# A hand-ordered selective scan: two copies moved behind the scans of their group, and the states of two tiles dealt anew among the engines

## The chip, the cores and the metric

The kernel runs on one core of a Trainium2 chip. The metric is the device time of one execution in microseconds (us); lower is better. The time stated for a kernel is the median of several executions.

## The reference

The network has four layers on a tensor of 4 images x 64 x 64 positions x 96 channels. Layers 0 and 1 are the costly ones: a group norm, an input projection to 192 + 192 channels, a depthwise 3x3 convolution with SiLU, a selective scan over the 4096 positions in four directions k, and a gated output projection. Layers 2 and 3 are linear attention and a small quantised feed-forward net on tokens.

The change lies in the selective scan. Cut to one image and one direction it computes, for 192 channels d and 16 states n:

```
x_dbl = xs @ x_proj_weight.T          # dts (6 ranks), B (16), C (16) of each position
delta = softplus(dts @ dt_w.T + bias)
for l in positions:                   # the recurrence, along the free dimension
    h[d, n] = exp(delta[l, d] * A[d, n]) * h[d, n] + delta[l, d] * u[l, d] * B[l, n]
    y[l, d] = sum_n h[d, n] * C[l, n]
y += D * u
```

## The kernel before

**Units, chunks, tiles, groups.** A unit is one layer and a pair of images; there are four units, one after another. The 2 x 192 channels of a pair are held as three tiles of 128 partitions: tile 0 and tile 1 are the first 128 channels of each image, tile 2 holds the last 64 of both. The 4096 positions of a direction are cut into four chunks of T = 1024, so a unit has 4 directions x 4 chunks = 16 chunks, and a chunk has three tiles. `steps` lists (k, ci, j): direction, chunk, tile. The 16 states of a tile are worked in groups of NG = 2, so a tile has eight groups, with n0 = 0, 2, ..., 14, and a chunk 24.

**What one state costs.** The scan itself is one VectorE (DVE) instruction over 1024 positions, which needs the decay `da` = exp(delta x A) from ScalarE (ACT), and the input `bp` = delta x u x B, in PSUM. Who makes `bp` is set for each tile and state by a letter of `MAKERS`:

- A: ACT scales the eight 128x128 blocks of the transposed delta x u (`dut`) by B (function `outer`, the tile `x`; in tile 2 sixteen blocks of 64 columns), and TensorE (PE) transposes them into `bp`.
- V: PE spreads B over the partitions with two selection matmuls (`bp<-bparts,sel`), and DVE multiplies `bp` by `du` in place just ahead of the scan.
- G: B is spread by a DMA (`bb`), GpSimd (POOL) multiplies it by `du` into `dbu`, and ACT writes the decay into `bp` instead (`exp_of`, held back in `late` to the next group's start).

After the scan POOL copies the last state where a later chunk follows (`last`), and multiplies h by C, which a DMA has spread (`cb`, three buffers, 1 MB a group). PE then transposes the products and adds them up in PSUM (`add_up`, `yp`), LAG = 3 groups later.

**The order.** Four engines run in program order, which is written out by hand in the loop over groups of `scan`. At group g it is: `bp` of the group's second state, the sum of group g - 3, ACT's work for group g + 1 (`start_ahead`: `x` and `da`; buffers: `x` 2, `da` 4, `bp` 2, `h` 4), the scan of the first state, the first `bp` of group g + 1, the scan of the second state, then the pieces that are due, then POOL's copies and products.

**The pieces.** The next chunk's projection (`project`, into the rows `cdt` and `crow`, and B in `bt` and `bparts`), the softplus of its deltas (`soften`) and the next tile's `du` and `dut` (`discretise`) are generators. Each yields the place at which its next piece is due, and `drive` runs the pieces of the place that has come. A projection's places are (tile, n0). In tiles 0 and 1 it makes one half of 512 positions each: a matmul `xps` at n0 = 8, 10 and 12, and at n0 = 14 ACT's copy of `xps` to `cdt` (76x512); behind the second copy the `crow` rows are written to memory. In tile 2 it turns B, and ends with ACT's copy `bparts` at n0 = 14. The places of `discretise` are 6, 8, 10 and 12.

`drive` is called behind the scans of each group. In the group with n0 = 14 it is also called once ahead of `start_ahead`, for `discretising` and `projecting`, so the last piece of a tile's projection stands ahead of ACT's work for the next tile's first group.

All engine instructions are recorded by one helper, so the profile shows them all under L61; they are told apart by their tiles.

Of the kernel before, what the change touches and what calls it, by code (L numbers as in the profile page):

```python
# [25 lines left out]
NS = 16  # L26
# [8 lines left out]
NG = 2  # L35
LAG = 3

MAKERS = ("VAAAVAAGVAVVAAVA", "AAVAVAVAAGAVAVAA", "VAVAVGVVVAVGVVAA")
NT = L // 128
STARTS = (0, 26, 52, 77)  # L40
HID = 4 * C
# [86 lines left out]
class Rounds:  # L128
# [7 lines left out]
    def run(self):  # L136
        for r in range(max(self.tasks) + 1):
            for task, args in self.tasks.get(r, ()):
                task(*args)
            yield  # L140

def between_scans(tc, cst, ident, half, pn, u, before, scan, after):

    with ExitStack() as stage:
# [374 lines left out]
def load_weights(nc, pk, w, k):  # L519

    wx = pk.tile([128, 3, NC], F32, name="wx")
    nc.sync.dma_start(out=wx, in_=w["wx"][k])
    wdt = pk.tile([NC, 3, 128], F32, name="wdt")
    nc.sync.dma_start(out=wdt, in_=w["wdt"][k])
    return wx, wdt

class PairScan:
# [129 lines left out]
    def scan(self, stage, nc):  # L657
# [9 lines left out]
        def begin_project(k, ci):  # L667
            return self.project(nc, nc.gpsimd, odd if ci % 2 else self.pq, pm, "m1", k, ci)

        def begin_discretise(at):  # L670
            return self.discretise(nc, nc.gpsimd, odd if at % 2 else self.pq, pm, "m0", at)

        def begin_soften(ats):
            return self.soften(nc, [self.pq, odd, odd, odd], pm, [("m0", "m1"), ("yp",), ("m0", "m1")], ats)
# [8 lines left out]
        def drive(pieces, place):  # L683

            while pieces and pieces[0] == place:
                pieces[0] = next(pieces[1])
# [4 lines left out]
        def maker(g, i):  # L691
            at, n0 = groups[g]
            return MAKERS[steps[at][2]][n0 + i]

# [7 lines left out]
        def start_ahead(g):  # L702

            at, n0 = groups[g]
            das, xs = {}, {}
            for i in range(NG):
                if maker(g, i) == "A":
                    xs[i] = outer(g, i)
                if maker(g, i) != "G":
                    das[i] = p2.tile([128, T], F32, name="da", bufs=4)  # L710
                    exp_of(das[i], g, i)
                if i == 0 and late:
                    exp_of(*late.pop())
            return das, xs
# [13 lines left out]
        def start_cb(g):  # L728

            at, n0 = groups[g]  # L730
            cb = p2.tile([128, NG, T], F32, name="cb", bufs=3)
            spread(cb, projected[at // 3][2], steps[at][2], n0)
            return cb
# [3 lines left out]
        def start_bb(g):  # L737

            at, n0 = groups[g]
            for i in range(NG):  # L740
                if maker(g, i) == "G":
                    bbs[g, i] = p2.tile([128, 1, T], F32, name="bb", bufs=1)
                    spread(bbs[g, i], projected[at // 3][2], steps[at][2], 2 * NS + n0 + i)

        def start_dbu(g):
            out = {}
            for i in range(NG):
                if (g, i) in bbs:
                    out[i] = p2.tile([128, T], F32, name="dbu", bufs=1)
                    nc.gpsimd.tensor_tensor(out[i], made[groups[g][0]][1], bbs.pop((g, i))[:, 0], ALU.mult)  # L750
            return out

        def start_bp(g, i, xs):

            at, n0 = groups[g]
            _, _, j = steps[at]
            bp = pm.tile([128, T], F32, name="bp", bufs=2)
            if maker(g, i) == "G":
                if g + 1 < len(groups):
                    late.append((bp, g, i))  # L760
                else:
                    exp_of(bp, g, i)
            elif maker(g, i) == "A":
                for t in range(T // 128):
                    nc.tensor.transpose(bp[:, 128 * t : 128 * t + 128], xs[i][:, t], ident)
            else:
                chosen = sel[:, n0 + i]
                if j < 2:
                    chosen = chosen[:, D1 * j : D1 * j + 1].to_broadcast([NP, 128])
                for hf in range(2):  # L770
                    cols = slice(512 * hf, 512 * hf + 512)
                    nc.tensor.matmul(
                        bp[:, cols],
                        chosen,
                        projected[at // 3][1][:, cols],
                        start=True,
                        stop=True,
                    )
            return bp
# [47 lines left out]
        def load_kept(at):  # L827

            if steps[at][0]:
                kept[at] = p2.tile([128, T // 128, 128], F32, name="kept", bufs=1)  # L830
                for tile_, there in places(at, kept[at]):
                    nc.sync.dma_start(out=tile_, in_=there)

        def finish_sum(at):
            tile_ = self.pq.tile([128, T // 128, 128], F32, name="ysum", bufs=1)
            nc.scalar.copy(tile_, sums.pop(at))
            for tile_, there in places(at, tile_):
                nc.sync.dma_start(out=there, in_=tile_)
# [6 lines left out]
        def sum_of(g):  # L845
            for i in range(NG):
                add_up(g, i, hs[g])
            del hs[g]

        def begun(pieces):  # L850
            return [next(pieces), pieces]

        for g, (at, n0) in enumerate(groups):
            k, ci, j = steps[at]
            rev, first, final = k >= 2, ci == 0, ci == L // T - 1
            if n0 == 0:
                if first and j == 0:
                    last = [pk.tile([128, NS], F32, name=f"last{i}", tag=f"last{i}") for i in range(3)]
                    for then in ORDER[ORDER.index(k) + 1 :][:1]:
                        weights[then] = load_weights(nc, pk, w, then)  # L860
                if j == 0:
                    projecting = begun(begin_project(*steps[at + 3][:2])) if at + 3 < len(steps) else []
                ahead_of = range(at + 1, min(at + (4 if at else 3), len(steps)))
                softening = begun(begin_soften(ahead_of)) if ahead_of and (j == 2 or at == 0) else []
                discretising = begun(begin_discretise(at + 1)) if at + 1 < len(steps) else []
            if n0 == 8 and at + 1 < len(steps):
                load_kept(at + 1)
            (da, xs), cb, dbu = ahead, cb_next, dbu_next
            if g + 2 < len(groups):
                start_bb(g + 2)  # L870


            def scan_one(i):
                if maker(g, i) == "V":
                    nc.vector.tensor_tensor(bps[i], made[at][1], bps[i], ALU.mult)
                way = slice(None, None, -1) if rev else slice(None)
                nc.vector.tensor_tensor_scan(
                    h[:, i, way],
                    (da[i] if i in da else bps[i])[:, way],
                    (bps[i] if i in da else dbu[i])[:, way],  # L880
                    0.0 if first else last[j][:, n0 + i : n0 + i + 1],
                    ALU.mult,
                    ALU.add,
                )

            bps = [bp_next, start_bp(g, 1, xs)]
            if g >= LAG:
                sum_of(g - LAG)
            if n0 == NS - NG:
                drive(discretising, n0)  # L890
                drive(projecting, (j, n0))
            if g + 1 < len(groups):
                ahead, cb_next, dbu_next = start_ahead(g + 1), start_cb(g + 1), start_dbu(g + 1)
            hs[g] = h = p2.tile([128, NG, T], F32, name="h", bufs=LAG + 1)
            scan_one(0)
            if g + 1 < len(groups):
                bp_next = start_bp(g + 1, 0, ahead[1])
            scan_one(1)
            drive(discretising, n0)
            if n0 == NG * (LAG - 1) and at > 0:  # L900
                finish_sum(at - 1)
            drive(softening, n0)
            drive(projecting, (j, n0))
            if not final:
                nc.gpsimd.tensor_copy(last[j][:, n0 : n0 + NG], h[:, :, 0] if rev else h[:, :, T - 1])
            for i in range(NG):
                nc.gpsimd.tensor_tensor(h[:, i], h[:, i], cb[:, i], ALU.mult)
# [445 lines left out]
```

## Time and profile before

| | |
|---|---|
| median of 3 executions | 10014.68 us (9996.38 to 10015.51) |
| the profiled execution | 10004.74 us, span 10003.0 us |
| granted TensorE clock | 0.93 of full speed |
| scan stretches of the four units | 2188.9, 2192.5, 2188.9, 2197.5 us |
| stretches before, between and after them | 172.3, 187.1, 186.2, 178.1, 511.5 us |
| chain that ended last, by engine | ACT 44%, PE 20%, DVE 18%, issue 13%, POOL 4% |

An engine's busy time is the union of its instructions. The groups of instructions give, behind the bar, busy us and the mean ns of one, and then the idle time of the engine just before them with what ended it. A mean of instructions that overlap (ACT's, PE's) is longer than the distance from one start to the next. PE is the matmuls, PEld the weight loads.

### The profile page before, as it was taken

Reading aid. Unit: us, or ns where it says so; the run is one execution under the profiler, and the core shown is the slowest. Engines: PE = TensorE matmul, PEld = TensorE weight load, DVE = VectorE, ACT = ScalarE, POOL = GpSimd, SP = SyncE. Lnnn points to the kernel's source line nnn. Section 1 sums busy time; section 2 is a strip of 40 time slices with the busy share of each in tenths; the row PEclk is TensorE's granted clock in tenths of the full one; section 3 lists DMA queues with packets and bytes.
Section 4 is the critical chain, followed back from the end, with each engine's and each line's share of the span. In section 5 each row is a group of like instructions: output and inputs, shape, how many; then the busy total and the mean of one; then the engine's idle time right before and its main releaser. Section 6 shows DMA issues by size and latency. Waiting matters only on the chain.

```text
span 10003.0 us, 148154 instructions
## 1 busy us (share of the span) xinstructions
PE 7800.2 (78%) x49548; PEld 5838.4 (58%) x49548; DVE 9336.2 (93%) x6794; ACT 9103.3 (91%) x21129; POOL 9004.9 (90%) x5362
## 2 busy tenths in 40 slices
PE   7778877777778888777877887777777888777766
PEld 4665655555566555555466555655566655555565
DVE  8999999998999999999899999999899999999957
ACT  6999999998899999998899999999899999999877
POOL 2999999996899999999599999999689999999946
PEclk8999999999899999999899999999989999999988
DMA  3777777776577877777577777777757777777730
GB/s 123 216 219 225 226 224 225 226 230 201 183 214 221 226 226 226 227 222 221 171 215 216 224 228 225 226 227 225 205 190 218 214 225 224 225 228 224 221 95 26
DMA packets 893171, 2083.68 MB, mean 208 GB/s; under 512 B 328278, under 2 KB 637848, under 8 KB 694776
## 3 DMA queue, kind: packets, MB, share of 16 engines
q1 hardware_dynamic: 892408, 2074.20, 70.7%
q8 instruction: 395, 6.47, 0.3%
q14 instruction: 368, 3.01, 0.1%
HBM read 1912.47 MB, written 161.48 MB: 207 GB/s over the span
## 4 chain that ended last, share of the span: by engine, by line
ACT 44%; PE 20%; DVE 18%; issue 13%; POOL 4%; DMA 1%; SPq 0%; DVEq 0%; ACTq 0%; POOLq 0%
ACT x L61 21%; ACT da L61 13%; DVE h L61 11%; PE yp L61 8%; PE bp L61 5%; DVE bp L61 4%; PE xps L61 3%; POOL h L61 2%; PE dps L61 2%; DVE vps L61 1%; ACT bp L61 1%; ACT ysum L61 1%; POOL du L61 1%; PE dpss L61 1%; ACT delta L61 1%
## 5 line engine op out<-in xcount | busy, mean ns | idle before, releaser
L61 POOL TENSOR_TENSOR h<-h,cb 128x1024 f32<-128x1024 f32 x3072 | 7197.0, 2369 | 165.8 <-DVE h L61 25.6
L61 DVE TENSOR_TENSOR_SCAN h<-da,last,bp 128x1024 f32<-128x1024 f32 x2112 | 4839.0, 2334 | 115.2 <-PE bp L61 7.5
L61 ACT ACTIVATE x<-dut,bt 128x128 f32<-128x128 f32 x14848 | 4225.5, 375 | 0.5 <-PE bp L61 0.3
L61 ACT ACTIVATE da<-delta,amat 128x1024 f32<-128x1024 f32 x2816 | 3150.9, 1144 | 17.4 <-DVE h L61 14.0
L61 PE MATMUL yp<-ident,h 128*128 128x128 f32 x24576 | 3156.2, 285 | 0.0
L61 PEld LDWEIGHTS yp<-ident,h 128*128 128x128 f32 x24576 | 2968.3, 148 | 210.0 <-issue 139.4
L61 PE MATMUL bp<-ident,x 128*128 128x128 f32 x12288 | 1779.2, 289 | 1210.2 <-DVE h L61 864.6
L61 PEld LDWEIGHTS bp<-ident,x 128*128 128x128 f32 x12288 | 1427.8, 147 | 1833.2 <-ACT x L61 1171.4
L61 DVE TENSOR_TENSOR bp<-du,bp 128x1024 f32<-128x1024 f32 x1280 | 1547.8, 1209 | 119.5 <-PE bp L61 119.3
L61 DVE TENSOR_TENSOR_SCAN h<-da,bp 128x1024 f32<-128x1024 f32 x704 | 1573.6, 2274 | 67.6 <-ACT da L61 19.7
L61 PE MATMUL bp<-bparts,sel 96*128 96x512 bf16 x2560 | 820.9, 404 | 559.5 <-DVE h L61 557.0
L61 PEld LDWEIGHTS <-sel 96*128 96x128 bf16 x2560 | 214.9, 101 | 937.4 <-DVE h L61 624.9
L61 POOL TENSOR_TENSOR dbu<-du,bb 128x1024 f32<-128x1024 f32 x256 | 606.6, 2370 | 0.0
L61 PE MATMUL xps<-u,wx 128*76 128x512 f32 x768 | 559.5, 814 | 0.0
L61 ACT ACTIVATE bp<-delta,amat 128x1024 f32<-128x1024 f32 x256 | 284.9, 1113 | 261.1 <-DVE h L61 261.1
L61 POOL TENSOR_TENSOR du<-delta,u 128x1024 f32<-128x1024 f32 x188 | 496.4, 2641 | 0.0
L61 DVE TENSOR_TENSOR_SCAN h<-bp,last,dbu 128x1024 f32<-128x1024 f32 x192 | 447.5, 2331 | 7.6 <-ACT bp L61 5.8
L61 POOL COPY last<-h 128x2 f32<-128x2 f32 x1152 | 217.3, 189 | 261.4 <-DVE h L61 156.0
L61 DVE SCALAR_TENSOR_TENSOR vps<-img,par,vps 128x512 f32<-128x512 f32 x520 | 387.0, 752 | 44.7 <-ACT vps L61 29.9
L61 PE MATMUL yp<-kept,ident 128*128 128x512 f32 x576 | 353.4, 747 | 65.2 <-ACT ysum L61 65.2
L61 PE MATMUL dups<-ident,du 128*128 128x128 f32 x1536 | 240.9, 280 | 63.9 <-POOL du L61 49.5
L61 ACT COPY ysum<-yp 128x1024 f32<-128x1024 f32 x192 | 192.4, 1002 | 101.3 <-PE yp L61 101.2
(146 smaller groups left out, 6092.8 us busy)
## 6 DMA issues: line engine op xcount, KB each, us to landing
cb<-crow SPq DMA_DIRECT2D x1024, 1024.0 KB
cb<-crow SPq DMA_DIRECT2D x1024, 512.0 KB
bb<-crow SPq DMA_DIRECT2D x128, 512.0 KB
bb<-crow SPq DMA_DIRECT2D x256, 256.0 KB
y<-ysum SPq DMA_DIRECT2D x192, 256.0 KB
kept<-y SPq DMA_DIRECT2D x160, 256.0 KB
y<-ysum SPq DMA_DIRECT2D x64, 512.0 KB
zt<-zg SPq DMA_DIRECT2D x64, 384.0 KB
```

What stands on the lines that cost most here:

```text
L61: return self.tc.keep_in_program_order(getattr(self.engine, op)(*args, **kwargs))
```

## The change

The copies of `cdt` in tiles 0 and 1 at n0 = 14 are no longer made ahead of `start_ahead`, but by the `drive` behind the scans of the same group. In tile 2 the early call for the projection stays. The early call for `discretising` goes. Two strings of `MAKERS` change: in tile 0 the two V of states 10 and 11 trade places with the two A of states 12 and 13, the counts staying at 9 A, 6 V, 1 G; in tile 1 the letters are dealt anew, from 10 A, 5 V, 1 G to 11 A, 4 V, 1 G. In groups of two states:

```
tile 0 before  VA AA VA AG VA VV AA VA
tile 0 after   VA AA VA AG VA AA VV VA
tile 1 before  AA VA VA VA AG AV AV AA
tile 1 after   VA AA VA AV AG AV AA AA
```

```diff
-MAKERS = ("VAAAVAAGVAVVAAVA", "AAVAVAVAAGAVAVAA", "VAVAVGVVVAVGVVAA")
+MAKERS = ("VAAAVAAGVAAAVVVA", "VAAAVAAVAGAVAAAA", "VAVAVGVVVAVGVVAA")
...
             bps = [bp_next, start_bp(g, 1, xs)]
             if g >= LAG:
                 sum_of(g - LAG)
-            if n0 == NS - NG:
-                drive(discretising, n0)
+            if j == 2 and n0 == NS - NG:
                 drive(projecting, (j, n0))
             if g + 1 < len(groups):
                 ahead, cb_next, dbu_next = start_ahead(g + 1), start_cb(g + 1), start_dbu(g + 1)
```

## The prediction

> **What bounds the kernel now.** I read four views: the page's busy line, the busy time in four consecutive chunks (stretches), the groups of instructions by shape, and the timelines of ACT, DVE and POOL around one wait.
>
> ```profile
> PE 7800.2 (78%) x49548; PEld 5838.4 (58%) x49548; DVE 9336.2 (93%) x6794; ACT 9103.3 (91%) x21129; POOL 9004.9 (90%) x5362
> ```
>
> Three engines are over 90% busy, so the page alone names no bound. The four scan stretches take 2188.9 to 2197.5 us each, 8768 of the 10003.0 us of the span, and hold all that the change touches. Four chunks (one direction) of the third one, from the first POOL product of one chunk to that of the next:
>
> ```profile
> core 0: us, PE busy (x) PEld busy (x) DVE busy (x) ACT busy (x) POOL busy (x), PEclk, DMA share, GB/s
> 5481.70:5617.90 136.20, 109.53 (x694) 79.62 (x694) 130.09 (x70) 128.34 (x303) 134.09 (x80) 0.95 0.75 219
> 5617.90:5755.20 137.30, 109.66 (x694) 80.33 (x694) 132.90 (x70) 128.97 (x306) 134.18 (x81) 0.95 0.79 224
> 5755.20:5891.40 136.20, 108.47 (x692) 79.85 (x690) 132.04 (x69) 128.02 (x302) 133.97 (x80) 0.95 0.77 226
> 5891.40:6028.30 136.90, 110.16 (x694) 82.22 (x695) 133.36 (x71) 129.24 (x306) 130.42 (x59) 0.94 0.81 233
> ```
>
> In the first three chunks POOL is busy all but 2 to 3 us, which is some 80 instructions with 0.03 us between them: **POOL is full there**. In the fourth, the last of a direction, POOL has no copies of last states (24 x 0.19 us less) and is idle 6.5 us; DVE with 133.4 busy sets the pace. How POOL waits there:
>
> ```profile
> 5471.28 7.02 POOL L61 TENSOR_TENSOR h<-h,cb 128x1024 f32<-128x1024 f32 x3 [0.87 <-DVE h L61]
> 5481.47 0.18 POOL L61 COPY last<-h 128x2 f32<-128x2 f32 x1 [3.17 <-DVE h L61]
> ```
>
> So POOL and DVE take turns: DVE's scans run 0.3 to 5 us ahead of POOL's products, and the lead is used up at two places of a chunk, tile 1 state 4 and the end of tile 2. ACT is ahead of both, and loses time like this at the end of tiles 0 and 1 (in brackets: idle before, and what ended it):
>
> ```profile
> 3132.34 0.58 ACT L61 COPY dut<-dups 128x512 f32<-128x512 f32 x1
> 3135.47 0.58 ACT L61 COPY cdt<-xps 76x512 f32<-76x512 f32 x1 [2.55 <-PE xps L61]
> 3135.95 2.45 ACT L61 ACTIVATE x<-dut,bt 128x128 f32<-128x128 f32 x8
> ```
>
> The eight x activations behind the copy needed nothing from PE. The groups give the prices and the sum of that wait:
>
> ```profile
> L61 POOL TENSOR_TENSOR h<-h,cb 128x1024 f32<-128x1024 f32 x3072 | 7197.0, 2369 | 165.8 <-DVE h L61 25.6 <-issue 21.8 <-DMA cb<-crow 9.6
> ...
> L61 ACT ACTIVATE da<-delta,amat 128x1024 f32<-128x1024 f32 x2816 | 3150.9, 1144 | 17.4 <-DVE h L61 14.0 <-POOL gn_norm L61 2.6
> L61 ACT ACTIVATE x<-dut,bt 128x128 f32<-128x128 f32 x9728 | 2970.8, 395 | 0.5 <-PE bp L61 0.3
> ...
> L61 DVE TENSOR_TENSOR bp<-du,bp 128x1024 f32<-128x1024 f32 x1280 | 1547.8, 1209 | 119.5 <-PE bp L61 119.3
> ...
> L61 ACT COPY cdt<-xps 76x512 f32<-76x512 f32 x128 | 74.5, 582 | 222.0 <-PE xps L61 222.0
> ```
>
> **What the Trainium skill says.** "PSUM — Partial Sum Buffer", section "Engine vs sequencer instructions": ScalarE's, VectorE's and GpSimd's queues are strict FIFO. The trace agrees: the x activations above stood 2.55 us behind a copy that they don't depend on. "ScalarE: Activation LUTs", section "What ACT_TABLE_LOAD costs": an activation with one pointer operand takes about 280 + 0.833 N ns, and neighbours overlap by 93; for N = 128 I estimate 294 ns from start to start, 2.35 us for eight. The trace agrees: 3135.95 to 3138.30, 2.35 us. "SBUF — State Buffer", section "Who interferes with whom": a VectorE instruction with at most one input in SBUF does not contend with GpSimd. DVE's product and scan each read one of their two tensors from PSUM here. The trace agrees: all 3072 POOL products lie between 2336 and 2495 ns. So fewer DVE products make POOL's no shorter.
>
> **The change, part by part.** There are 64 chunks (4 units of 16).
> 1. *The copy of cdt in tiles 0 and 1* goes behind the next group's ACT work. Removed: waits of 222.0 us, 3.5 a chunk (117 of 128 copies waited). A wait is put in its place only if PE's xps is later than the next group's ACT work, and that includes a da whose buffer (ring of four) is freed by the scan of state 13; xps stands ahead of that. I take 0. Bounds: 3.5 saved, none saved. Behind the later copy in tile 1 stand the write of crow (SP) and the dps matmuls (PE, two groups on, about 10 us). The write went out at 3183.03; a copy some 4 us later moves it to about 3187; the first reader of crow is the next chunk's cb, eight groups of 4.9 us away, 39 us. If that cover went, POOL would stand by the excess. What SP has behind crow, cb and bb of the next groups, is held by POOL freeing cb's ring of three in any case (3186.72). POOL's own queue is not touched.
> 2. *The first drive of discretising* at n0 = 14 finds no piece with that place (they are 6, 8, 10, 12): nothing goes.
> 3. *Tile 1: state 13 from V to A*, by count (5 V become 4, 10 A become 11). DVE loses one product: 1.21 busy, 1.3 us from its start to the next scan's, 64 x 1.3 = **83 us of DVE**. ACT gains eight x: 2.34 x 64 = **150 us of ACT**; the da exists either way. PE gets eight transposes (0.87 us) for two selections (0.44): +0.43 a chunk, 28 us, beside 1422 us in which PE waited with bp for DVE.
> 4. *The order in tiles 0 and 1*: counts up to tile 0 state 13 and up to tile 1 state 9 stay what they were; only at tile 0 states 10 and 11 two x sets (4.7 us) come one group earlier. DVE runs 4.5 to 5 us ahead of POOL there. Zero, with bounds of a gain or loss of 0.3 us a chunk (DVE's waits for ACT's da there are of that size).
>
> ACT's account: -3.5 + 2.3 = -1.2 us a chunk. Its lead over DVE, by the timelines: da of tile 1 state 13 is ready 6.7 us before its scan, state 15 3.9, tile 2 state 1 1.15. After: the last gains 2.5 and 1.5 (both waits), loses 2.34 (x) and 1.3 (DVE earlier), and stands at 1.5. So ACT should still lead.
>
> DVE's account: -1.3 a chunk. In the first three chunks POOL is full: of their POOL waits of 0.2, 1.1 and 0.4 us (DVE late) about 1.2 go, the rest of DVE's gain becomes lead. In the fourth POOL waits 6.4 us (0.87 and 3.17 above, the rest in between): DVE's own 1.3 goes, and of the lead built before it 1 to 2.5 us; a lead of over some 7 us stops at PE, which takes sums of h three groups back from POOL before the next bp. Together 3.5 to 5, say 4.5 us in four chunks: 16 x 4.5 = **72 us**. The two engines meet next at POOL, at 540 us in four chunks.
>
> **How the numbers follow.** The profiled execution took 10004.7 us, 1.7 around its span; 10004.7 - 72 = 9933. The median shown, 10014.7, is 10 above it and the fastest, 9996.4, 8 below, so I name 9935. A measurement of this kernel can tell about 0.2%, 20 us, from no change.
>
> - **Forecast, 0.65**: 45 to 130 us less; 130 is all of POOL's waits, 8.0 in four chunks x 16.
> - **Rival 1, hidden behind POOL, 0.20**: the lead gained is lost again (to PE's bp, for which DVE already waits 119 us, or to ACT's G states, which wait 261 us for DVE); only the 16 last chunks gain their 1.3. For it: POOL is full in three of four. Against: the lead is at 0.3 at the pinches, so any gain there shows at once. 16 x 1.3 = 21 us less: 9984, give or take 20.
> - **Rival 2, slower, 0.15**: ACT becomes the bound in tile 1. Its last groups are AV, AA, AA: ACT 4.4 + 6.8 + 6.8 = 18.0 us against DVE's 5.7 + 4.4 + 4.4 = 14.5. If ACT cannot keep the 2.5 us from tile 0 (da's ring of four and x's of two hold it two groups ahead) and those waits turn into waits for DVE, the 2.34 us land on DVE's path: 2.34 - 1.3 = +1.0 a chunk, 64 us, 10069. It decides when ACT's lead at tile 1 state 12 is under 2.3 us. For it: ACT works without a break through tile 1 today (3135.47 to 3177.9). Against: the lead of 6.7 us above.
> - That the change doesn't do what it says holds for part 2 alone.
>
> Faster by over 0.2% has nearly all of the forecast and half of rival 1 less a little, 0.72; slower nearly all of rival 2, 0.13; the rest 0.15. The range, 9870 to 10020, leaves out most of rival 2 and the ends.
>
> **What would show it.** In the profile after: cdt's idle of 222 us gone to under 20; x at 15360 activations, bp<-du,bp at 1216; ACT's busy time up by 150 us, DVE's down by 77, POOL's the same to 5 us; POOL's wait for DVE at the end of each direction 3.2 down to about 1. It is wrong if DVE's waits for ACT's x or da in tile 1 grow by over 1 us a chunk (rival 2), or if DVE's waits for PE's bp grow by what it saved (rival 1).

## The result, and the profile after

| | before | after |
|---|---|---|
| median of 6 executions | 10012.5 us | 10054.9 us |
| range | 9996.4 to 10023.7 | 10025.4 to 10069.5 |
| the profiled execution, its span | 10004.7, 10003.0 | 10057.1, 10055.3 |
| granted TensorE clock | 0.930 | 0.919 |

The ratio is 1.004, with a 95% interval of 1.003 to 1.005: the change costs 42 us, where I forecast a gain of 72. The busy line of the page after:

```profile
PE 7987.5 (79%) x49932; PEld 5978.5 (59%) x49932; DVE 9282.4 (92%) x6730; ACT 9260.8 (92%) x21641; POOL 9010.5 (90%) x5362
```

ACT is busy 157 us more (150 forecast), DVE 54 less (77 forecast), POOL the same to 6. **PE is busy 187 us more**, where the transposes were to add 28. The groups of instructions by shape, after:

```profile
L61 ACT ACTIVATE x<-dut,bt 128x128 f32<-128x128 f32 x10240 | 3129.5, 395 | 104.5 <-PE bp L61 104.4
...
L61 DVE TENSOR_TENSOR bp<-du,bp 128x1024 f32<-128x1024 f32 x1216 | 1473.3, 1212 | 226.9 <-PE bp L61 226.2
...
L61 ACT COPY cdt<-xps 76x512 f32<-76x512 f32 x128 | 73.7, 576 | 16.5 <-PE xps L61 16.5
```

The wait for xps is gone (222.0 to 16.5), and DVE's products cost 74.5 us less. But x, which hardly waited (0.5 us), now waits 104.5 us for PE, and DVE's wait for PE's bp ahead of its products has grown from 119.3 to 226.2: by more than DVE saved. The same four chunks of a direction as shown of before, by stretches:

```profile
core 0: us, PE busy (x) PEld busy (x) DVE busy (x) ACT busy (x) POOL busy (x), PEclk, DMA share, GB/s
5530.20:5672.80 142.60, 116.34 (x700) 84.44 (x699) 129.46 (x69) 130.92 (x311) 134.37 (x81) 0.90 0.73 210
5672.80:5810.20 137.40, 110.21 (x700) 80.85 (x699) 132.07 (x69) 131.34 (x313) 134.31 (x80) 0.95 0.77 224
5810.20:5946.70 136.50, 110.68 (x698) 82.15 (x697) 131.49 (x68) 130.73 (x311) 134.01 (x79) 0.94 0.78 225
5946.70:6083.30 136.60, 110.67 (x700) 82.54 (x701) 132.16 (x70) 131.40 (x313) 130.47 (x58) 0.94 0.77 234
```

Three chunks are where they were (137.3, 136.2 and 136.9 before). The first takes 142.6 instead of 136.2 us, at a clock of 0.90 instead of 0.95. So most of the loss sits in single chunks, and those are slow on PE.

**Inside the slow chunk.** `dps` and `dpss` are the PSUM tiles in which PE makes the next deltas (`soften`); these matmuls contract over 12 rows of `cdt`, where the transposes use all 128. PE's timeline at the start of tile 2, after:

```profile
5617.55 1.43 PE L61 MATMUL bp<-ident,x 128*128 128x128 f32 x3 [0.15 <-ACT x L61]
5618.77 3.62 PE L61 MATMUL yp<-ident,h 128*128 128x128 f32 x16
5622.19 1.06 PE L61 MATMUL bp<-bparts,sel 96*128 96x512 bf16 x2
5623.18 3.78 PE L61 MATMUL dps<-cdt,wdt 12*128 12x512 f32 x4
5626.89 3.67 PE L61 MATMUL yp<-ident,h 128*128 128x128 f32 x16
```

Four dps take 3.78 us and sixteen yp 3.67. In before's same chunk:

```profile
5573.48 1.98 PE L61 MATMUL dps<-cdt,wdt 12*128 12x512 f32 x4
5575.40 1.97 PE L61 MATMUL yp<-ident,h 128*128 128x128 f32 x16
```

The clock (the column after POOL; 1.00 is full, 0.50 half clock) in slices of 3.4 us, the step in which the trace's clock records change; after:

```profile
5613.90:5617.30 3.40, 1.61 (x10) 0.77 (x8) 3.40 (x3) 3.40 (x13) 3.32 (x4) 1.00 1.03 222
5617.30:5620.70 3.40, 3.24 (x14) 2.56 (x14) 3.27 (x2) 3.40 (x8) 3.32 (x3) 0.50 1.03 224
5620.70:5624.10 3.40, 3.40 (x11) 2.08 (x11) 2.00 (x2) 3.05 (x3) 3.40 (x3) 0.50 1.02 259
5624.10:5627.50 3.40, 3.40 (x7) 1.28 (x6) 3.27 (x3) 0.01 (x1) 3.32 (x3) 0.50 0.98 211
5627.50:5631.00 3.50, 3.50 (x17) 2.94 (x15) 1.62 (x1) 0.40 (x1) 3.50 (x3) 0.50 1.02 225
5631.00:5634.40 3.40, 2.98 (x7) 1.11 (x7) 3.07 (x2) 3.37 (x5) 3.32 (x3) 1.00 0.65 140
```

and before, the same place:

```profile
5565.80:5569.20 3.40, 1.25 (x8) 0.79 (x9) 3.40 (x3) 3.40 (x15) 3.40 (x2) 1.00 1.02 268
5569.20:5572.60 3.40, 3.40 (x17) 3.09 (x16) 3.27 (x3) 3.40 (x5) 3.32 (x3) 0.50 1.04 229
5572.60:5576.00 3.40, 3.40 (x17) 1.72 (x15) 3.27 (x3) 1.90 (x3) 3.40 (x3) 1.00 1.01 217
```

In both a slice with PE idle for over half of it (1.61 and 1.25 us busy) is followed by half clock. Before, one full slice brings the clock back. After, **it stays at half for four slices, 13.7 us, though PE is busy all but 0.2 us of it**; ACT stands 6.48 us for yp in it, and DVE 1.40 and 2.18 us for bp.

The Trainium skill, "TensorE: Matmul & The Clock Gate", section "Part 1: The HAM clock gate", says that the clock is set by how busy PE has been in windows of 3413 ns. The trace agrees on the window: its clock records fit a period of 3413.3 ns. But "busy" doesn't explain the three full slices at half clock. I cut the traces into these windows and weighted each matmul's time in a window with the share of the 128 rows that it uses; call that the row share. Take the windows at full clock in which PE was busy for over 95%: half clock followed 57 of 610 in before and 46 of 691 in after. All but one of these in each had a row share under 0.45, and no such window with a share under 0.45 kept the full clock (56 of 56 and 45 of 45 fell).

Two bounds fitted to before and after, a share under 0.45 to fall from full clock and over about 0.8 to rise from half, give 99 and 97% of the decisions at full clock, and 98 and 95% of those at half; bounds on plain busy time, fitted in the same way, give 97 and 95%, 94 and 87%. (To guess always the same gives 89 and 88%, 68 and 63%.) The bounds are not the whole rule: of the windows at full clock with a share of 0.5 to 0.7, 2 of 723 fell in before, but 45 of 712 in after.

Of the three half-clock slices above that half clock follows, the second and third have PE busy throughout and row shares of 0.67 and 0.27. The first, with 0.95, is one of the misses, and five more of after's long stretches begin in the same way.

### The profile page after: what moved, and what is told of

It reads as the page before. It is cut to its first block, busy times and chain, and to the rows that moved or that the text cites. A ratio compares the mean times of both kernels' runs of the same rounds, so it can differ in the third digit from the quotient of the medians.

```text
span 10055.3 us, 149326 instructions
## 1 busy us (share of the span) xinstructions
PE 7987.5 (79%) x49932; PEld 5978.5 (59%) x49932; DVE 9282.4 (92%) x6730; ACT 9260.8 (92%) x21641; POOL 9010.5 (90%) x5362
## 4 chain that ended last, share of the span: by engine, by line
ACT 59%; PE 15%; DVE 10%; POOL 7%; issue 7%; DMA 1%; SPq 0%; DVEq 0%; POOLq 0%; ACTq 0%
ACT x L61 31%; ACT da L61 18%; DVE h L61 6%; PE yp L61 5%; POOL h L61 5%; PE bp L61 3%; PE dps L61 2%; ACT bp L61 2%; DVE bp L61 1%; ACT ysum L61 1%; DVE vps L61 1%; ACT dut L61 1%; POOL du L61 1%; PE xps L61 1%; ACT L61 1%
## 5 line engine op out<-in xcount | busy, mean ns | idle before, releaser
L61 ACT ACTIVATE x<-dut,bt 128x128 f32<-128x128 f32 x15360 | 4384.2, 376 | 104.5 <-PE bp L61 104.4
L61 PE MATMUL yp<-ident,h 128*128 128x128 f32 x24576 | 3214.9, 288 | 0.0
L61 PEld LDWEIGHTS yp<-ident,h 128*128 128x128 f32 x24576 | 3025.1, 150 | 205.8 <-issue 139.2
L61 PE MATMUL bp<-ident,x 128*128 128x128 f32 x12800 | 1922.5, 289 | 1127.7 <-DVE h L61 631.2
L61 PEld LDWEIGHTS bp<-ident,x 128*128 128x128 f32 x12800 | 1500.0, 146 | 1847.8 <-ACT x L61 1351.9
L61 DVE TENSOR_TENSOR bp<-du,bp 128x1024 f32<-128x1024 f32 x1216 | 1473.3, 1212 | 226.9 <-PE bp L61 226.2
L61 PE MATMUL bp<-bparts,sel 96*128 96x512 bf16 x2432 | 797.3, 412 | 437.0 <-DVE h L61 433.5
```

The source lines that it names most:

```text
L61: return self.tc.keep_in_program_order(getattr(self.engine, op)(*args, **kwargs))
```

## The experiments

Two theories stood against each other: **C**, the clock at tile 2's start, and **A**, too little time on ACT or in PE's queue for the eight extra x and transposes a chunk. A third, **M**, was the late copy itself. Times are medians, ratios are against before on the same chip (before's medians: 10017 in the first four, 10014 in the next four, 10004 in the last).

**e1_move**: the diff's loop, the old `MAKERS` (the move).

> The copy of cdt moved, the makers as before. Theory C (clock): the loss of the change is TensorE's clock, which stays at half for 10 to 14 us at the start of tile 2 in 12 of 64 chunks, some 5.5 us each; whether it does depends on how busy PE is just ahead of the dps matmuls, which the new letters of tile 1 alter. Then the move alone shows at most a few chunks over 141 us and lies within 20 us of before, 9990 to 10020. Theory A (ACT or PE's queue is short of time because of the eight extra x and transposes a chunk): the move alone, without the extra A, is faster than before by 20 to 60 us, 9950 to 9990. Theory M (the late copy itself does the harm, through crow on SP and dps on PE): as slow as after, 10040 to 10060.

Measured: 10006 us, ratio 0.9992 (0.9984 to 1.0001). The move neither harms nor helps by what can be told: M falls, and A's gain of 20 to 60 us isn't there.

**e2_makers**: the new `MAKERS`, the old loop.

> The new makers, the copy of cdt where it was. Theory C: chunks over 141 us again, in no number that I can derive; 10020 to 10080. Theory A: ACT keeps its wait of 3.5 us a chunk for xps and gets 2.3 us of x on top, so slower than after by 1 us a chunk or more, 10100 to 10160. Theory M: near before, 10000 to 10030.

Measured: 10086 us, ratio 1.0068 (1.0053 to 1.0083). The loss comes with the letters. It is too small for A's figure and slightly above C's.

**e3_after_rows** and **e4_before_rows**: dps and dpss over all rows of cdt. The added weights are zero.

```diff
-                nc.tensor.matmul(ps, wdt[ND:, j], cdt[ND:, 512 * hf : 512 * hf + 512], start=True, stop=True)
+                nc.tensor.matmul(ps, wdt[:, j], cdt[:, 512 * hf : 512 * hf + 512], start=True, stop=True)
```

> After, with the dps and dpss matmuls over all 76 rows of cdt in place of 12 (the weights of the other 64 rows are zero, so the sum is the same). The two traces suggest that the clock is granted by the rows that PE works on: dps keeps PE busy but with 12 of 128 rows. Theory C: the long stretches at half clock at the start of tile 2 go, no chunk but a unit's first is over 140 us, and the time falls by 50 to 80 us, to 9970 to 10005. Theories A and M: nothing of theirs is touched, so within 15 us of after, 10040 to 10070.

> Before, with dps and dpss over all 76 rows. Theory C: before has four chunks slowed by a long stretch at half clock (some 3 us each) and three short ones of 3.4 us in every chunk; those at dps go: 10 to 40 us faster, 9970 to 10000. Theories A and M: same as before within 10 us.

Measured: e3 9955 us, ratio 0.9937 (0.9920 to 0.9954), **100 us less than after**, more than C's 50 to 80; e4 9978, ratio 0.9961 (0.9946 to 0.9976), 39 less than before. Nothing but the number of rows differs, and a matmul of 76 rows takes no longer (median 592 ns against 587). e3's slices at tile 2's start:

```profile
5542.70:5546.10 3.40, 1.33 (x7) 0.77 (x7) 3.27 (x3) 3.40 (x15) 3.40 (x2) 1.00 0.97 210
5546.10:5549.50 3.40, 3.37 (x15) 3.08 (x16) 3.40 (x2) 3.40 (x5) 3.32 (x4) 0.50 1.05 227
5549.50:5553.00 3.50, 3.50 (x20) 2.33 (x19) 2.76 (x3) 2.29 (x3) 3.50 (x2) 1.00 0.97 250
5553.00:5556.40 3.40, 2.90 (x14) 1.50 (x13) 3.40 (x3) 2.38 (x3) 3.32 (x3) 1.00 1.05 229
5556.40:5559.80 3.40, 3.38 (x10) 1.31 (x9) 3.37 (x4) 3.40 (x6) 3.32 (x4) 1.00 1.04 224
```

The idle slice and one half-clock slice are still there; the clock comes back behind it, and dps runs at full speed. Of the windows at full clock with PE busy for over 95%, none was followed by half clock any more (0 of 790 in e3, 0 of 673 in e4). C holds. And with 76 rows the change itself is faster: e3 takes 23 us less than e4, on the same chip, and each of its four executions took less than each of e4's.

**e5_tile0** and **e6_tile1**: after, with one of the two strings as before.

```diff
e5: -"VAAAVAAVAGAVAAAA"  +"AAVAVAVAAGAVAVAA"   (tile 1)
e6: -"VAAAVAAGVAAAVVVA"  +"VAAAVAAGVAVVAAVA"   (tile 0)
```

> After, with tile 1's letters as before: the copy moved, and only tile 0 dealt anew. Theory C1 (the long half-clock stretch is set off by tile 1's new end, groups AA and AA in place of AV and AA: PE transposes blocks one by one as ACT makes them, and idles in between, just ahead of dps): as the move alone, 9995 to 10020, with at most four chunks over 141 us apart from a unit's first. Rival C0 (tile 0's new order does it, shifting PE's pattern from there on): as slow as after, 10040 to 10070.

> After, with tile 0's letters as before: the copy moved, and only tile 1 dealt anew, with its extra A. Theory C1: as slow as after or slower, 10040 to 10080, chunks over 141 us. Rival C0: as the move alone, 9985 to 10015.

Measured: e5 10055 us, ratio 1.0038 (1.0023 to 1.0053); e6 10074, ratio 1.0062 (1.0045 to 1.0079). Each theory failed in one run, C1 in e5 and C0 in e6: either string alone brings the loss, though tile 0's only trades places and adds no work. So neither tile's new order is the one trigger, and A has nothing to offer for e5.

**e7_rows_crow**: e3, with the early call kept in tile 1.

```diff
-            if j == 2 and n0 == NS - NG:
+            if j > 0 and n0 == NS - NG:
```

> After with the 76 rows (9955 us), and tile 1's copy of cdt back ahead of the next group's ACT work, so that crow is written early and only tile 0's copy is moved. In the run with 76 rows POOL waits 24 us for cb's DMA, 2.1 us in each last chunk of a direction at tile 2 state 4, which it does not in before; before has 9.6 us. Theory S (the later write of crow holds up cb on SP's queue): these waits go below 10 us, and the time falls by 5 to 20 us against that run's 9955, if ACT's wait for xps in tile 1, some 1.5 us a chunk, is hidden. Rival: the DMA is late because POOL comes earlier there; then the waits stay, and the copy's wait costs 0 to 60 us: 9955 to 10010.

Measured: 9966 us, ratio 0.995 (0.9935 to 0.9965). POOL's product waits 8.9 us for cb's DMA instead of 23.8 (at tile 2 state 2, where most of it lies by the trace, 1.5 instead of 16.0): the later write of crow did hold up cb, as theory S says. The time did not fall for it; three long stretches at half clock came back. The intervals of its ratio and e3's overlap, so the 10 us are not settled.

**e8_move_rows**: move and 76 rows, the old letters.

> Move and 76 rows with the makers of before. With it the three edits can be set against each other. If the new makers are worth what DVE saves once the clock is out of the way (my prediction's 83 us of DVE, in part), this is slower than the run with all three, 9955, by 15 to 40 us: 9970 to 9990. If the new makers are worth nothing even so, it is within 10 us of it or faster: 9935 to 9965.

Measured: 9955 us, ratio 0.9941 (0.9926 to 0.9956), the same as e3. On top of the move and the 76 rows the new letters are worth nothing that can be told. But the clock's part is not gone from this comparison: e3's trace is at half clock for 1451 us, e8's for 1277.

**e10_makers_rows**: the new letters and 76 rows, the old loop.

> The new makers with the copy of cdt where it was, and 76 rows. The new makers alone were the slowest kernel (10086 us) with 24 chunks that held a stretch of 10 us or more at half clock. Theory C: its stretches go as well, and the time falls by 90 to 130 us to 9955 to 9995, so that the four kernels with 76 rows lie within 40 us of one another. Rival (ACT is short of time with the extra A when it still waits for xps): the 76 rows give no more than the 39 us that they gave before, 10040 to 10055.

Measured: 9972 us, ratio 0.9963 (0.9949 to 0.9977), 114 us less than e2 (105 by the ratios, as the two ran on different chips). The time is in C's range, and the rival's 10040 is excluded. But C's stretches did not all go: 6 of 24 are left. In each of the six, PE is busy throughout the first two windows at half clock, with row shares of 0.59 and 0.67 to 0.69: under the fitted bound of about 0.8 for a rise, as 76 of 128 rows are.

**Together.** Medians in us (runs on different chips are compared by their ratios above), and from each trace the chunks with a stretch of 10 us or more at half clock (of the 56 that are neither a unit's first nor its last), their mean length, and that of the others:

| | 12 rows | stretches: mean, others | 76 rows | stretches: mean, others |
|---|---|---|---|---|
| before | 10017 | 3: 139.8, 136.6 | 9978 | 0: 136.3 |
| move | 10006 | 2: 139.2, 136.6 | 9955 | 0: 135.9 |
| letters | 10086 | 24: 139.4, 136.9 | 9972 | 6: 139.9, 136.1 |
| both | 10055 | 10: 142.4, 136.8 | 9955 | 0: 136.1 |
| move, tile 0's letters | 10055 | 7: 140.6, 137.0 | | |
| move, tile 1's letters | 10074 | 13: 142.1, 136.9 | | |

With 12 rows most of what differs is how many chunks have a long stretch, but not all: the others take 136.6 to 137.0 us. For after against before, the stretches make 10 x 5.6 - 3 x 3.2 = 46 us, the level of all 56 chunks 10, and the units' first chunks 8; the rest of the span is 12 us shorter, which leaves the 52 between the two spans. In e5 the level (137.0 against 136.6) makes 25 us and the stretches 15. (The 12 chunks that the expectations name count two units' first ones; e4's four in before are three by this count.) The two fastest versions, e3 and e8, beat before and after alike.

## Why the prediction was wrong, point by point

- **What bounds the kernel**: right for three chunks of four (POOL full), and it still holds in after's chunks without a stretch. Of the 6.4 us that POOL waits in the fourth, only 4.3 were waits for DVE (3.2 and 1.1), so less stood to be gained than I counted. And I read the clock as one column that never changed, 0.94 to 0.95, and did not look inside a chunk, where before too falls to half for 3.4 us several times and in three chunks for 10 us.
- **Part 1, the move**: the 222 us of waits went (16.5 left). Behind the copy in tile 1 POOL's waits for cb's DMA grew, 25.0 us against 9.6. I had put this at nothing because SP's cb behind crow was held by POOL's buffers in any case; e7 shows that the late write makes most of it. The removed wait bought nothing that can be told by itself (e1, 0.9992): most of ACT's time went into other waits, in e1:

```profile
ACT bp L61 <- DVE h L61: 371.2, 160, 5.0
ACT ysum L61 <- PE yp L61: 152.0, 115, 10.8
ACT x L61 <- PE bp L61: 24.0, 61, 0.7
```

  Before, these were 261, 101 and 0.3. With 76 rows the move may be worth some 20 us (e4 0.9961, e8 0.9941, intervals that overlap).
- **Part 3, DVE's 83 us**: the product's part came (74.5), and the step that failed is the next one, that it becomes lead and shortens POOL's waits. DVE waits for PE's bp instead, after:

```profile
DVE bp L61 <- PE bp L61: 226.2, 185, 3.5
```

  That was rival 1's mechanism, and it goes with PE's clock: 209 of the 226 us are waits during half clock or within one window behind it, against 102 of 119 before, so all of the growth is there. From e8 to e3, with 76 rows, this wait grows too:

```profile
DVE bp L61 <- PE bp L61: 43.6, 45, 3.9
DVE bp L61 <- PE bp L61: 108.6, 161, 3.6
```

  94 of e3's 109 us lie during or just behind half clock, so what the letters would be worth at a full clock stays open. A part of the lead did arrive: POOL's wait for DVE at the end of a direction, 3.2 before and forecast at about 1, is 2.7 in after and 2.0 in e3 (means of the 12 ends inside the units).
- **Part 3, PE's 28 us "beside 1422 us in which PE waited", costed at nothing**: the term that made the loss. PE had idle time, but its speed depends on how that time lies: PE's busy time rose by 187 us, and the time at half clock from 1399 to 1639 us.
- **Part 4, the order, zero within 0.3 us a chunk**: wrong. e5 holds tile 0's new order and the move alone and is at 1.0038, where the move alone is at 0.9992: some 46 us, 0.7 a chunk. I also overlooked that the first two groups of tile 1 change, from AA VA to VA AA.
- **Rival 2, slower by ACT**: right in sign, wrong in cause. ACT did not run short: in the slow chunk it is idle for 6.48 us, waiting for PE, and DVE's waits for ACT's da, which were to grow by over 1 us a chunk, went from 20 to 24 us in all.

The cause of the loss, half clock held by matmuls of few rows, is shown by the 76-row runs: with these rows filled up the change no longer loses. Why a given order of letters meets it in 2 or 24 chunks is not shown; that small shifts of PE's work against the windows of 3.413 us decide it is my guess.

## What to carry to other kernels

Idle time of PE is not free room: look at the granted clock in slices of a few us around each PE wait before costing a change of order at nothing, and expect a re-dealing of work to move it. Where a matmul contracts over few rows, fill it up with rows whose weights are zero if they lie at hand: here it took no time, and was worth 39 us to the kernel before and 100 to the one after. A wait that is removed from an engine off the path can turn up under another name, as ACT's did here; ask first for whom that engine was late.

## What the runs showed of the hardware

In these traces TensorE's clock follows the rows in use, not busy time alone. A window of 3.41 us that PE fills at full clock, but with a row share under 0.45 (dps with 12 of 128 rows), was followed by half clock each time, 56 times in before and 45 in after; with 76 rows in the same matmuls, which take 592 ns against 587, no filled window was.

The clock is slower to come back than to go. With a row share of 0.5 to 0.7, 721 of 723 windows of before kept the full clock, and all 56 at half clock stayed at half; a rise takes about 0.8. The bounds are fitted to the traces of before and after, were not tested one by one, and leave a part of the decisions open.
